# A fused transformer and state-space kernel: where the weighted values and the first out products of a group stand between the gate's halves

## The chip, the cores and the metric

The kernel runs on one core of a Trainium2 chip. The metric is the device time of the whole program in microseconds (us), as the median of three runs. The engines are named as in the profile: PE is the matrix engine (PEld its weight loads), DVE the vector engine, ACT the scalar engine, POOL the GpSimd engine, SP the engine that issues nearly all DMAs. Each engine has its own instruction queue and works it off in order; engines wait for each other by semaphores.

## The reference, cut to what matters

Four residual layers on 1024 tokens of 512 features: attention, a gated feed-forward layer, a Mamba-2 mixer, and the feed-forward layer again. The change touches only the mixer:

```python
def _L0_attn_b_ref(input_states, in_proj_w, conv_w, conv_b, dt_bias, A_log, D, norm_w, out_w):
    H, P, N, G, K = (128, 64, 128, 8, 4)
    INTER = H * P                                    # 8192 channels
    proj = input_states @ in_proj_w.T
    gate, xBC, dt = ...                              # split of proj
    xBC = silu(conv(xBC) + conv_b)                   # 4 taps along the tokens
    hs, Bm, Cm = ...                                 # values, keys, queries (8 groups)
    y = _ssd(hs, -exp(A_log), Bm, Cm, D, dt, dt_bias)
    g = y * silu(gate)
    gg = g.reshape(b, l, G, INTER // G)
    g = gg * rsqrt(mean(gg * gg, -1) + EPS) * norm_w # one norm for each group
    return g @ out_w.T
```

The kernel computes `_ssd` for each sequence of 256 tokens as a masked, decayed attention: (C B^T, times a decay of the two positions) times (dt x), plus D x.

## The kernel before, in words

The mixer's 8192 channels are 64 blocks of 128 channels (two heads each), in 8 groups g of 8 blocks. Block i is number gi = i mod 8 of its group. All tiles have channels on the 128 partitions and the 1024 tokens (4 sequences of 256) along the free axis. Every product with weights is made of three matmuls per slice of 128 features (`mm3`, L110, matmuls at L115 to L117), since each operand is split into a high and a low part (`split`: ACT casts at L107, the other engine subtracts at L108).

A block does this:

- `projected("x", i)` (L1127): 24 matmuls into a PSUM tile `pp`, in two halves of 512 tokens with 12 matmuls each. Between the halves it calls the function `between`, which is empty for x. `pp` has two buffers, used in turn by the x and the gate of each block.
- `conv` (L961): ACT scales the last tap into `acc`, DVE adds three taps (L971), ACT applies silu (L975). The result is `x2`, with two buffers.
- `projected("g", i, between)`: the gate's two halves, with `between` in the middle; ACT writes silu of it into `gt` (L1204), which has one buffer.
- `differences` (L999) for two heads: the decay factors `em` (four buffers, so two blocks' worth), made of DVE (L1004), POOL (L1008) and ACT (L1013 to L1016) work from rows `r` that SP loads.
- `turned` (L1022): eight PE transposes of `x2` into `trx` (L1027), and DVE multiplies by dt into `xd` (L1030).
- `weighted` (L1019): DVE multiplies `em` by the group's masked scores `gm` (L1020).

What needs all this comes one block later. `inner_products(i - 1)` (L1160) gives the weighted values of the block before: `product` (32 matmuls into `pyy`, L1044), and `gated` (DVE adds D x and multiplies by the gate, L1054 and L1057; SP stores the result to DRAM as `spill`, L1059; ACT squares it, L1066; POOL adds the square to the group's sum `sq`, L1067). The square is written into the block's `x2`, so that buffer is free for the convolution two blocks on only when POOL has read it.

Once a group: `scores` (L978) is a generator. Its first step makes the tile `gm`; each of the next four makes the scores of one sequence, with two products on PE (L986 and L990, each shown as two matmuls) into a tile `pg`, and a masking multiply by DVE into `gm` (L991).

The out products of group g are made during group g+1, for 8 tiles of 128 tokens. `recall` (L1097) loads half the group's stored values for one tile from DRAM (`gr`) and splits it into `gh`, which has three buffers; two recalls make a tile. `outer` (L1150) makes 24 matmuls (`pog`), 12 with each half; for the first tile (t = 0) it also computes the norm with `root` (L1085: 16 small matmuls `pqs`, a square root on ACT at L1093, a reciprocal on DVE at L1094); then DVE adds the scaled result to `x` (`scaled`, L1115). `PER` says how many tiles are recalled at the end of the block before block gi.

`pog`, `pqs`, `pg` and `trx` all come from one PSUM pool of two buffers (L797, tag "m").

From block 8 on PE's order is exactly that of the program text, written out by hand (`manual_schedule`, L1227). For the other engines the framework's planner orders the instructions: it goes by the order of the text, but puts a later instruction ahead where an earlier one is not ready by its own plan. What it decides is fixed when the program is built.

In the first block of a group (gi = 0, g > 0) PE's order before the change is: x; the scores of two sequences; first half of the gate; the scores of the other two; the weighted values of the block before; second half of the gate; transposes. In the second block: x; the out product of t = 0 with its norm; the weighted values; the out product of t = 1; both halves of the gate; transposes. Blocks 2 to 7: x; one out product; the weighted values; the gate; transposes (and, in two of them, the projection of the next group's B or C).

Of the kernel before, what the change touches and what calls it, by code (L numbers as in the profile page):

```python
# [79 lines left out]
def hybrid_kernel(  # L80
# [705 lines left out]
    def mixer(feed, later):  # L786
        with ExitStack() as es, ExitStack() as inner:
# [173 lines left out]
            def conv(pp, ch, tag, bufs):  # L961

                acc = (po_ if tag == "gb" else p2).tile([P, NT], F32, name="acc", tag=tag, bufs=bufs)
                nc.scalar.activation(  # L964
                    acc, pp, AF.Identity, bias=cb_s[:, ch : ch + 1], scale=cw_s[:, ch, 3:4]
                )
                av = acc.rearrange("p (b t) -> p b t", b=B)
                pv = pp.rearrange("p (b t) -> p b t", b=B)
                for tap in range(3):
                    d = 3 - tap  # L970
                    nc.vector.scalar_tensor_tensor(  # L971
                        av[:, :, d:], pv[:, :, : L - d], cw_s[:, ch, tap : tap + 1], av[:, :, d:],
                        ALU.mult, ALU.add,
                    )
                silus.append(nc.scalar.activation(acc, acc, AF.Silu).ins)  # L975
                return acc

            def scores(bt, ct):  # L978

                gm = p2.tile([P, B, 3, P], F32, name="gm", tag="gm", bufs=1)  # L980
                yield gm
                for b in range(B):
                    pg = ps.tile([P, 3, P], F32, name="pg", tag="m")
                    k0, k1 = bt[:, b * L : b * L + P], bt[:, b * L + P : (b + 1) * L]
                    q1 = ct[:, b * L + P : (b + 1) * L]
                    nc.tensor.matmul(  # L986
                        pg[:, 0:2, :].rearrange("p s i -> p (s i)"), k0, ct[:, b * L : (b + 1) * L],
                        start=True, stop=True,
                    )
                    nc.tensor.matmul(pg[:, 2, :], k1, q1, start=True, stop=True)  # L990
                    nc.vector.tensor_tensor(gm[:, b], pg, tri.rearrange("p (s i) -> p s i", s=3), ALU.mult)  # L991
                    yield

            def rows(h):
                r = p2.tile([P, NT], F32, name="r", tag="r", bufs=2)
                load(r, cumd[h : h + 1, :].to_broadcast([P, NT]))
                return r
# [40 lines left out]
            def product(xd, es2):  # L1038
                py = ps_y.tile([P, B, L], F32, name="pyy", tag="pyy")
                for b in range(B):  # L1040
                    for k in range(2):
                        for hh in range(2):
                            d = slice(hh * PD, (hh + 1) * PD)
                            nc.tensor.matmul(  # L1044
                                py[d, b, k * P :], xd[:, 2 * b + k, d],
                                es2[hh][:, b, 2 * k : 2 if k == 0 else 3, :].rearrange("p s i -> p (s i)"),
                                start=(k == 0), stop=(k == 1),
                            )
                return py

            def gated(n, x2, gt, py, sq):

                gb = po_.tile([P, NT], F32, name="gb", tag="gb", bufs=3)
                nc.vector.scalar_tensor_tensor(  # L1054
                    gb, x2, dh[:, n : n + 1], py.rearrange("p b t -> p (b t)"), ALU.mult, ALU.add
                )
                nc.vector.tensor_tensor(gb, gb, gt, ALU.mult)  # L1057
                if n < NB - 1:
                    load(spill[(n // GB) % 2][n % GB], gb)  # L1059
                else:  # L1060
                    last.append(gb)
                if sq is None:
                    sq = p2.tile([P, NT], F32, name="sq", tag="sq")
                    nc.scalar.activation(sq, gb, AF.Square)
                else:
                    nc.scalar.activation(x2, gb, AF.Square)  # L1066
                    (nc.gpsimd if n < NB - 1 else nc.vector).tensor_tensor(sq, sq, x2, ALU.add)  # L1067
                return sq
# [16 lines left out]
            def root(sq):  # L1085
                pq = ps.tile([P, TT], F32, name="pqs", tag="m")
                for t in range(TT):
                    nc.tensor.matmul(
                        pq[:, t : t + 1], sq[:, t * P : (t + 1) * P], ones[:, 0:1], start=True, stop=True
                    )  # L1090
                rg = rg_s.pop(0)
                rg_s.append(rg)
                nc.scalar.activation(rg, pq, AF.Sqrt, bias=eps, scale=1.0 / (GB * P))  # L1093
                nc.vector.reciprocal(rg, rg)  # L1094
                return rg
# [13 lines left out]
            def partial(po, g, hl, half):  # L1109
                ks = range(half * 4, half * 4 + 4)  # L1110
                mm3(po, [[v[:, k % 4, :] for v in hl] for k in ks], [wos[g][k] for k in ks],
                    half == 0, half == 1)

            def scaled(g, t, po):
                nc.vector.scalar_tensor_tensor(  # L1115
                    x[:, t, :], po, rgs[g][:, t : t + 1], x[:, t, :], ALU.mult, ALU.add
                )
# [32 lines left out]
            def outer():  # L1150

                q, t, hl = recalled.pop(0)
                po = ps.tile([P, C], F32, name="pog", tag="m")
                for half in range(2):
                    partial(po, q, hl[half], half)
                if t == 0:
                    rgs[q] = root(sqs.pop(q))
                scaled(q, t, po)

            def inner_products(m):  # L1160
                px2, gt, xd, em = stage.pop(m)
                py = product(xd, em)
                sqs[m // GB] = gated(m, px2, gt, py, sqs.get(m // GB))
# [3 lines left out]
            scoring = scores(group["b"], group["c"])  # L1167
# [3 lines left out]
            rr = {h: rows(h) for h in range(2)}  # L1171
            stage, sqs, wos, rgs, todo = {}, {}, {}, {}, []
            recalled = []
            PER = {1: 2, 2: 1, 3: 1, 4: 1, 5: 1, 6: 1, 7: 1}
            def block(i, scoring, gm):
                g, gi = divmod(i, GB)
                x2 = conv(projected("x", i), i, "x2", 2)
                if gi == 0 and g:

                    scoring = scores(group["b"], group["c"])  # L1180
                    gm = next(scoring)
                    next(scoring)
                    next(scoring)
                    todo.extend((g - 1, t) for t in range(TT))
                outers = len(recalled)
                if outers:
                    outer()
                if i and (outers or g == 0):
                    inner_products(i - 1)
                while recalled:  # L1190
                    outer()
                if gi == 7:
                    wos.setdefault(g, []).extend(out_weights(g, k) for k in range(4))

                def between():

                    for _ in scoring:
                        pass
                    if not outers and g:
                        inner_products(i - 1)  # L1200

                pp = projected("g", i, between)
                gt = p2.tile([P, NT], F32, name="gt", tag="gt", bufs=1)
                nc.scalar.activation(gt, pp, AF.Silu)  # L1204
                em = []
                for h in (2 * i, 2 * i + 1):
                    with tc.issue_after(silus[2]) if i == 0 else ExitStack():
                        em.append(differences(h, rr.pop(h)))
                    if h + 2 < H:
                        rr[h + 2] = rows(h + 2)  # L1210
                xd = turned(i, x2)
                if gi in NEXT and g + 1 < G:
                    convolved(NEXT[gi], g + 1)
                for e in em:
                    weighted(e, gm)
                stage[i] = (x2, gt, xd, em)
                for _ in range(PER.get(gi + 1, 0)):
                    if todo:
                        q, t = todo.pop(0)
                        recalled.append((q, t, [recall(q, t, half) for half in range(2)]))  # L1220
                if gi == 7:
                    wos[g].extend(out_weights(g, k) for k in range(4, 8))
                return scoring, gm

            for i in range(GB):
                scoring, gm = block(i, scoring, gm)
            with tc.manual_schedule(engines={nc.tensor.engine}):  # L1227
                for i in range(GB, NB):
                    scoring, gm = block(i, scoring, gm)
# [122 lines left out]
```

## Time and profile before

| what | value |
|---|---|
| median of three runs | 1916.23 us (1913.35 to 1919.33) |
| the profiled execution's own time | 1920.11 us |
| its span, first to last instruction | 1918.3 us |
| PE busy | 1819.3 us |
| DVE busy | 1468.6 us |
| ACT busy | 1462.1 us |
| POOL busy | 389.3 us |
| mean granted PE clock | 0.978 |

The span is the time from the first to the last instruction of one profiled execution. "Busy" leaves out waits, register work and the issuing of DMAs. Rows of a timeline give the start, the duration, the engine, the line, the operation, the tile written and the tiles read, and in brackets the idle time before it with what ended it. Matmuls overlap: a 512-column matmul is listed with 0.39 us, but one starts every 0.23 us. Group 2 (blocks 16 to 23, from 730.6 us) serves as the example below; its first block ends its x projection at 736.15 us.

### The profile page before, as it was taken

To read this page: it belongs to the slowest core of one execution; us is meant where nothing else is said; L and a number is where in the kernel's file an instruction comes from. 1 tells how busy PE (TensorE), PEld (TensorE's weight loads), DVE (VectorE), ACT (ScalarE), POOL (GpSimd) and SP (SyncE) were. 2 spreads that over 40 slices of the span, in tenths; PEclk is the share of its full clock that TensorE was granted. 3 is DMA by queue.
4 is the path that set the end of the run, shared out by engine and by line. 5 is a ranking of instruction groups with operands and counts; after the bars stand their busy time and mean duration, and the time that the engine had idled before them with its cause. 6 is when DMAs were issued, how large, how long until landed. Compare 5 with 4: busy or idle time off the path is not lost.

```text
span 1918.3 us, 29873 instructions
## 1 busy us (share of the span) xinstructions
PE 1819.3 (95%) x10706; PEld 1465.5 (76%) x10706; DVE 1468.6 (77%) x2304; ACT 1462.1 (76%) x2877; POOL 389.3 (20%) x393
## 2 busy tenths in 40 slices
PE   8999989899989999999999989999999999999997
PEld 6777767677767887888788878877788788778776
DVE  5566667789997788778877787878777877777767
ACT  5666675379987888787878787887788788778753
POOL 6332230024411112121211111111111121111100
PEclk8999999899999999999999999999999999999999
DMA  4000000034554445444544454445445544554241
GB/s 141 1 1 1 22 15 25 24 111 154 182 180 160 159 143 175 149 151 125 192 148 154 137 177 140 162 144 171 148 143 165 165 143 143 163 167 149 94 139 49
DMA packets 152773, 240.35 MB, mean 125 GB/s; under 512 B 12464, under 2 KB 77616, under 8 KB 152624
## 3 DMA queue, kind: packets, MB, share of 16 engines
q1 hardware_dynamic: 152624, 238.44, 38.6%
q8 instruction: 84, 1.38, 0.3%
q14 instruction: 65, 0.53, 0.1%
HBM read 202.75 MB, written 35.65 MB: 124 GB/s over the span
## 4 chain that ended last, share of the span: by engine, by line
PE 74%; ACT 10%; DVE 8%; DMA 3%; POOL 2%; issue 2%; SPq 0%; DVEq 0%; ACTq 0%; POOLq 0%
PE pp L115 12%; PE pp L116 11%; PE pp L117 11%; PE pyy L1044 8%; PE pog L115 6%; PE pog L117 6%; PE pog L116 6%; PE trx L1027 2%; ACT e L477 2%; DMA wor<-in_wout_dram 2%; DVE acc L971 1%; POOL sq L1067 1%; PE ptr L493 1%; PE pq L115 1%; PE pq L116 1%
## 5 line engine op out<-in xcount | busy, mean ns | idle before, releaser
L115 PE MATMUL pp<-mx,w 128*128 128x512 f32 (+1 forms) x1160 | 464.2, 400 | 3.2 <-DVE acc L971 1.1
L117 PE MATMUL pp<-mx,w 128*128 128x512 f32 (+1 forms) x1160 | 452.5, 390 | 0.0
L116 PE MATMUL pp<-mx,w 128*128 128x512 f32 (+1 forms) x1160 | 452.4, 390 | 0.0
L971 DVE SCALAR_TENSOR_TENSOR acc<-pp,cw_s,acc 128x1012 f32<-128x1012 f32 (+2 forms) x240 | 304.4, 1271 | 18.4 <-ACT acc L964 16.7
L1020 DVE TENSOR_TENSOR em<-em,gm 128x1536 f32<-128x1536 f32 x128 | 241.5, 1888 | 73.7 <-ACT em L1016 73.7
L115 PEld LDWEIGHTS pp<-mx,w 128*128 128x128 f32 x1160 | 218.9, 189 | 55.9 <-issue 9.7
L117 PEld LDWEIGHTS pp<-mx,w 128*128 128x128 f32 x1160 | 218.6, 188 | 46.2 <-issue 0.7
L116 PEld LDWEIGHTS pp<-mx,w 128*128 128x128 f32 x1160 | 219.2, 189 | 40.8 <-issue 0.6
L1008 POOL TENSOR_SCALAR_AFFINE_SELECT r<-r 128x512 f32<-128x512 f32 x128 | 94.8, 741 | 759.9 <-DMA r<-cumd 587.8
L115 PE MATMUL pog<-wo,gh 128*128 128x512 f32 x512 | 207.0, 405 | 30.1 <-ACT gh L107 28.3
L1067 POOL TENSOR_TENSOR sq<-sq,acc 128x1024 f32<-128x1024 f32 x55 | 152.7, 2776 | 374.3 <-ACT acc L1066 374.3
L117 PE MATMUL pog<-wo,gh 128*128 128x512 f32 x512 | 204.7, 400 | 0.6 <-DVE gh L108 0.6
L116 PE MATMUL pog<-wo,gh 128*128 128x512 f32 x512 | 204.3, 399 | 0.0
L1044 PE MATMUL pyy<-em,xd 128*64 128x128 f32 (+1 forms) x2048 | 183.7, 329 | 1.3 <-DVE em L1020 1.0
L1044 PEld LDWEIGHTS pyy<-em,xd 128*64 128x64 f32 x2048 | 130.1, 137 | 57.6 <-issue 17.6
L1013 ACT ACTIVATE em<-r,col_t 128x128 f32<-128x128 f32 x512 | 170.5, 390 | 0.8
L1016 ACT ACTIVATE em<-r,col_t 128x128 f32<-128x128 f32 x512 | 166.3, 389 | 0.2
L1004 DVE TENSOR_SCALAR em<-r,col_t 128x128 f32<-128x128 f32 x512 | 138.8, 328 | 22.8 <-PE pyy L1044 18.4
L108 DVE TENSOR_TENSOR w<-wr,w 128x512 fp32r<-128x512 f32 x126 | 93.3, 740 | 65.9 <-ACT w L107 65.9
L115 PEld LDWEIGHTS pog<-wo,gh 128*128 128x128 f32 x512 | 98.9, 193 | 55.0 <-ACT gh L107 31.2
L107 ACT CAST w<-wr 128x512 fp32r<-128x512 f32 x144 | 88.6, 616 | 64.7 <-PE pp L116 61.9
L107 ACT CAST gh<-gr 128x512 fp32r<-128x512 f32 (+1 forms) x128 | 76.4, 607 | 69.2 <-PE pog L116 55.9
(290 smaller groups left out, 3310.5 us busy)
## 6 DMA issues: line engine op xcount, KB each, us to landing
wr<-in_win_dram SPq DMA_DIRECT2D x287, 256.0 KB, 2.8
r<-cumd SPq DMA_DIRECT2D x128, 512.0 KB, 3.9
spill<-gb SPq DMA_DIRECT2D x63, 512.0 KB, 2.6
gr<-spill SPq DMA_DIRECT2D x120, 256.0 KB, 2.9
wor<-in_wout_dram SPq DMA_DIRECT2D x64, 256.0 KB, 3.0
out_dram<-x SPq DMA_DIRECT2D x8, 256.0 KB, 2.3
x<-in_x_dram SPq DMA_DIRECT2D x1, 1536.0 KB, 9.9
gr<-spill SPq DMA_DIRECT2D x8, 192.0 KB, 2.5
```

The source lines that it names most:

```text
L107: nc.scalar.copy(hl[0], v)
L115: nc.tensor.matmul(o, lh, rh, start=(first and k == 0), stop=False)
L116: nc.tensor.matmul(o, lh, rl, start=False, stop=False)
L117: nc.tensor.matmul(o, ll, rh, start=False, stop=(last and k == n - 1))
L971: nc.vector.scalar_tensor_tensor(av[:, :, d:], pv[:, :, : L - d], cw_s[:, ch, tap : tap + 1], av[:, :, d:], ALU.mult, ALU.add,)
L1004: nc.vector.tensor_scalar(e[:, b, 2, :], rv[:, b, 1, :], col_t[:, h, b, 1:2], 0.0, ALU.subtract, ALU.min,)
L1008: nc.gpsimd.affine_select(rv[:, :, 0, :], rv[:, :, 0, :], pattern=[[0, B], [1, P]], compare_op=ALU.is_ge, fill=-1e30, base=0, channel_mult ...
L1013: nc.scalar.activation(e[:, b, 1, :], rv[:, b, 1, :], AF.Exp, bias=col_t[:, h, b, 2:3])
L1016: nc.scalar.activation(e[:, b, 0, :], rv[:, b, 0, :], AF.Exp, bias=col_t[:, h, b, 0:1])
L1020: nc.vector.tensor_tensor(e, e, gm, ALU.mult)
L1044: nc.tensor.matmul(py[d, b, k * P :], xd[:, 2 * b + k, d], es2[hh][:, b, 2 * k : 2 if k == 0 else 3, :].rearrange("p s i -> p (s i)"), sta ...
L1067: (nc.gpsimd if n < NB - 1 else nc.vector).tensor_tensor(sq, sq, x2, ALU.add)
```

## The change

In the first two blocks of groups 1 to 7 (`late`), nothing stands between x and the first half of the gate any more. Between the gate's halves of the first block stand the scores of two sequences, the weighted values of the block before, and the scores of the other two sequences. Between the gate's halves of the second block stand the weighted values of the first, and behind them the out product of t = 0. The second block's end recalls two tiles instead of one, the first block's end one instead of two, so the third block has two out products, around its weighted values.

```diff
-            PER = {1: 2, 2: 1, 3: 1, 4: 1, 5: 1, 6: 1, 7: 1}
+            PER = {1: 1, 2: 2, 3: 1, 4: 1, 5: 1, 6: 1, 7: 1}
             def block(i, scoring, gm):
                 g, gi = divmod(i, GB)
                 x2 = conv(projected("x", i), i, "x2", 2)
                 if gi == 0 and g:
-
                     scoring = scores(group["b"], group["c"])
                     gm = next(scoring)
-                    next(scoring)
-                    next(scoring)
                     todo.extend((g - 1, t) for t in range(TT))
-                outers = len(recalled)
-                if outers:
-                    outer()
-                if i and (outers or g == 0):
-                    inner_products(i - 1)
-                while recalled:
-                    outer()
+
+
+                late = gi < 2 and g > 0
+                if not late:
+                    if recalled:
+                        outer()
+                    if i:
+                        inner_products(i - 1)
+                    while recalled:
+                        outer()
                 if gi == 7:
                     wos.setdefault(g, []).extend(out_weights(g, k) for k in range(4))
 
                 def between():
-
+                    if late:
+                        if gi == 0:
+                            next(scoring)
+                            next(scoring)
+                        inner_products(i - 1)
+                        while recalled:
+                            outer()
                     for _ in scoring:
                         pass
-                    if not outers and g:
-                        inner_products(i - 1)
 
                 pp = projected("g", i, between)
```

## The prediction, made before the changed kernel was run

> **What bounds the kernel now.** I read the page's busy line first, then PE's list of waits, then PE's timeline over one group's first two blocks, then the other engines over the same stretch.
>
> ```profile
> PE 1819.3 (95%) x10706; PEld 1465.5 (76%) x10706; DVE 1468.6 (77%) x2304; ACT 1462.1 (76%) x2877; POOL 389.3 (20%) x393
> PE pog L115 <- ACT gh L107: 28.3, 7, 4.8
> PE pg L986 <- DVE gm L991: 4.5, 6, 0.9
> ```
>
> PE is the bound. In the list of waits (engine and tile, what ended the wait, us in total, times, longest) the first place goes to seven waits of the out products for `gh`, one in each of groups 1 to 7; six waits of the scores stand second. Both lie in the blocks that the change reorders. PE's timeline of group 2:
>
> ```profile
> 740.66 0.38 PE L990 MATMUL pg<-acc 128*128 128x128 f32 x2
> 741.77 0.70 PE L986 MATMUL pg<-acc 128*128 128x256 f32 x2 [0.72 <-DVE gm L991]
> 742.30 0.38 PE L990 MATMUL pg<-acc 128*128 128x128 f32 x2
> 742.62 2.82 PE L1044 MATMUL pyy<-em,xd 128*64 128x256 f32 x32
> ...
> 757.07 0.39 PE L117 MATMUL pog<-wo,gh 128*128 128x512 f32 x1
> 761.32 0.50 PE L115 MATMUL pog<-wo,gh 128*128 128x512 f32 x1 [3.87 <-ACT gh L107]
> ...
> 763.33 0.63 PE L117 MATMUL pog<-wo,gh 128*128 128x512 f32 x1
> 763.76 0.63 PE L115 MATMUL pog<-wo,gh 128*128 128x512 f32 x1
> ...
> 766.03 1.84 PE L1088 MATMUL pqs<-ones,sq 128*128 128x1 f32 x16
> ```
>
> The second half of the first out product waits 3.87 us, and then matmuls start every 0.43 us instead of every 0.23. The stretches before, in and after the wait show why (stretch, length, busy times, then the granted clock):
>
> ```profile
> 757.30:761.30 4.00, 0.15 (x1) 0.00 (x0) 3.79 (x8) 3.97 (x6) 0.00 (x0) 1.00 0.50 171
> 761.30:765.50 4.20, 4.18 (x11) 2.96 (x12) 4.20 (x7) 4.03 (x10) 1.13 (x1) 0.62 0.77 243
> ```
>
> The clock is granted at about half for some 3.5 us behind the wait. From 754.57 to 766.03 this out product takes 11.46 us; undisturbed ones take 5.53. What is late is the group's own last block: its products end at 745.4, DVE finishes `gb` at 751.36, the spill lands at 753.96, the recall at 756.69, and ACT casts at 760.66 to 761.27, being held until then:
>
> ```profile
> 751.51 1.04 ACT L1066 ACTIVATE acc<-gb 128x1024 f32<-128x1024 f32 x1
> 753.87 1.03 ACT L1204 ACTIVATE gt<-pp 128x1024 f32<-128x1024 f32 x1
> 757.11 1.20 ACT L964 ACTIVATE acc<-pp,cb_s,cw_s 128x1024 f32<-128x1024 f32 x1 [2.21 <-POOL sq L1067]
> 760.66 1.12 ACT L107 CAST gh<-gr 128x512 fp32r<-128x512 f32 x2
> ```
>
> **What is removed.** PE does the same matmuls; the gain can only be waits and slow clock. The first out products of groups 1 to 7 take 11.21, 11.46, 11.37, 12.32, 11.83, 11.80 and 12.53 us. Less 5.53 each that is 5.68 + 5.93 + 5.84 + 6.79 + 6.30 + 6.27 + 7.00 = **43.8 us**: 28.9 idle (the row's 28.3, and 0.6 for DVE's low part), the rest slow clock. The third and fourth scores take 2.39 us in group 2 (740.23 to 742.62) and 1.39 in group 1, where they wait for nothing; 1.0 in each of six groups is **6.1 us** (group 4 has 1.16). Together 49.9.
>
> **The new order against the old times.** I lay PE's new order out without waits for group 2, from the end of x at 736.15, with durations from the same timeline: gate half 2.85, two scores 1.23, weighted values 2.75, two scores 1.39, gate half 2.88, transposes 0.79, x 5.54, gate half 2.85, weighted values 2.75, out product 2.76 + 2.77, norm sums 1.77, gate half 2.88. This gives the time at which PE will ask for each thing; beside it I set when the trace of before has it ready. That assumes that the other engines keep their times, a cautious reading, since the weighted values of block 15 end at 742.98 instead of 745.37.
>
> - Second scores, asked at 742.98: need the first masking multiplies. Before, DVE did the first 0.4 us after its scores, but the second only at 741.72. Bounds 0 to 1.0 a group (the wait of today); I take 0.3, since 2.75 us of weighted values lie between.
> - Gate half of block 17, asked at 753.58: needs the `pp` buffer of block 16's gate, which ACT releases with `gt` at 754.90. The two gate projections were 14.6 us apart in ordinary blocks (0.8 + 5.5 + 5.5 + 2.75) and are now 6.3. Bounds: 0 if `gt` follows the earlier `gb`, 1.3 in this group (up to 2.3 in group 7) if ACT keeps its order. I take 0.7.
> - Weighted values of block 16, asked at 756.43: the second multiply by `gm` ends at 754.22. 2.2 us of cover; before, 13.6.
> - Out product's second half, asked at 761.94: cast at 761.27. 0.7 to spare, plus whatever the earlier `gb` and the gate's wait add. **The 3.87 us wait is covered even if ACT does not move**, by a gate half and the weighted values (5.6 us) that now run ahead. Taken at nothing; were that cover gone, the old 5.9 come back.
> - Transposes, asked at 769.36: they use both "m" buffers, so `scaled` of the out product must be done within the 2.88 us of the gate half. Square root 0.27, reciprocal 0.20, `scaled` 0.74 sum to 1.2; before it took 6.1 us (767.80 to 773.87), 2.8 of them DVE idle ahead of the next weighted values, which now come first. Bounds 0 to 2.8; I take 0.5.
> - Third block, two out products: the stores they recall are long on DRAM; before, the t = 1 tile ran with no wait. The move takes two recall DMAs (256 KB each), four splits and one `scaled` along. In SP's queue the `wr` and `r` loads behind the recalls come forward; POOL's square sum and the block 17 convolution behind it start no later. Cost nothing: the blocks after it leave DVE 4 us in 20 idle (16.10 and 15.47 busy in two stretches of 20.2).
>
> New waits are 1.5 us a group, 10.5 in seven. They are too short for the half clock, by the 0.72 us row, after which nothing slows.
>
> **Two rules beside the rows.** The Trainium skill (GPSIMD Engine Reference, 8. Key points) says that GpSimd shares its SBUF interfaces with VectorE and contends with DVE instructions in a two-port mode or with two SBUF inputs. That speaks against the change: the square sum on POOL moves towards the multiplies by `gm`, the tightest cover above.
>
> ```profile
> 752.70 4.37 POOL L1067 TENSOR_TENSOR sq<-sq,acc 128x1024 f32<-128x1024 f32 x1 [6.83 <-ACT acc L1066]
> 752.47 1.75 DVE L1020 TENSOR_TENSOR em<-em,gm 128x1536 f32<-128x1536 f32 x1
> 754.74 3.40 DVE L1004 TENSOR_SCALAR em<-r,col_t 128x128 f32<-128x128 f32 x6
> L1020 DVE TENSOR_TENSOR em<-em,gm x128: 1742/1751/3015, 425.0 to 1813.4; 128x1536 f32<-128x1536 f32 x128
> ```
>
> Six 128-column pieces of `em` take 3.40 beside the square sum, 1.2 undisturbed; a multiply takes 3.0 at most instead of 1.75. By the row the multiply ends at 755.5, cost 0. By the rule at its worst (held for all 4.4 us, from 750.3) it ends at 756.5, 0.1 us late. I take 0.
>
> The other is TensorE: Matmul & The Clock Gate, Part 1: half clock only after an idle window of about 3.4 us. Here group 1 has a wait of 3.04 us (transposes for ACT's silu, 559.95 to 562.99), and the clock is 0.66 from 563 to 567; the next x takes 7.18 instead of 5.55. The row decides: a new wait of 3 us costs 1.6 more (7 × 4.6 = 32 instead of 7 × 3.0 = 21). That wait itself hangs on DVE and ACT work that the change leaves, and I let it stand.
>
> **Sum.** −43.8 − 6.1 + 10.5 = −39.4. On the profiled execution's 1920.1 that gives 1880.7. It lies 0.2% above the runs' median, so I apply the difference to the median: 1916.2 − 39.4 = **1877**.
>
> **Rivals.**
> 1. All new waits are covered since ACT and DVE follow the earlier weighted values: −49.9, 1866. For it: 2.4 us of lead. Against: DVE has 40.8 and ACT 39.5 busy us from 736.15 to 782.38, and PE will pass through that in about 7 us less than 46.2.
> 2. The planner leaves ACT's casts of `gh` behind later work, about 4 us later than now: the half is 2 us late with 1.9 of slow clock, which leaves 7.1 − 1.5 − 4.0 = 1.6 a group, −11, 1905. For it: the casts already stand behind a convolution that waits for POOL. Against: the recall stands ahead of that in the text.
> 3. **Slower**: DVE's planner puts block 17's three taps ahead of the second multiply of block 16. They wait for ACT and POOL and end at 764.23; the multiply then ends at 765.9, 9.5 us late, with 2.1 of slow clock. 7.1 saved against 11.6 lost is +4.5 a group, +31, 1948. It decides from a multiply that ends 5 us late, at 761.4. Against: the multiply stands ahead in the text and the trace keeps that order.
> 4. The waits only move and add up to about the same; PE's order does change, so this needs an accident.
>
> **Chances.** The forecast (1867 to 1892) 0.55; rival 1 at 0.17; rival 2 (1892 to 1910) 0.14; no change within 0.3%, 5.7 us, which is about what can be told from none, 0.04; slower 0.10. Faster is 0.86. The range runs from 1862 (rival 1 with group 1's 3 us wait gone) to 1905, in rival 2; its own case alone would give 1867 to 1892.
>
> **What would show it.** Right: the out products' waits for `gh` gone from the list; first out products at 5.5 us and the clock whole behind them; short waits at the second block's gate for `gt` (L1204) and at its transposes; group period 5 to 7 us shorter. Wrong: waits of `pyy` for `em` (L1020) above 3 us in the second block, or `gh` waits still there.

## The result, and the profile after

The changed kernel takes **1885.71 us** (median of four runs, 1883.82 to 1887.02), beside 1915.66 for the kernel before in the same session; the ratio is 0.9841, with a 95% interval of 0.9823 to 0.9859. That is 30 us faster, where 39 were forecast, and inside the forecast's 1867 to 1892. The profiled execution took 1886.09 us with a span of 1884.3 and a mean granted clock of 0.987.

The page's busy line, and the four lines of PE's list of waits that the change touches (engine and tile, what ended the wait, us in total, times, longest), of the kernel after:

```profile
PE 1805.5 (96%) x10706; PEld 1454.6 (77%) x10706; DVE 1475.8 (78%) x2304; ACT 1470.4 (78%) x2883; POOL 385.5 (20%) x393
PE pg L986 <- DVE gm L991: 14.4, 7, 4.6
PE trx L1027 <- DVE gm L991: 2.1, 5, 1.0
PE trx L1027 <- ACT rg L1093: 1.4, 1, 1.4
PE trx L1027 <- DVE x L1115: 1.2, 4, 0.4
```

The line of the out products that wait for `gh`, 28.3 us in seven waits, is gone. The scores that wait for their masking multiplies have taken its place: seven waits again, but half the time. Of the transposes' lines those for `rg` and `x` are new; the one for `gm` had one wait of 1.1 us before, ahead of the blocks that changed, and it is still there. PE's busy time fell by 13.8 us for the same 10706 matmuls: that part of the gain is slow clock that no longer follows the waits.

PE's timeline of group 2 after (start, duration, engine, line, tiles, and in brackets the idle time before it and what ended it); its first x projection ends at 730.77:

```profile
734.14 0.60 PE L986 MATMUL pg<-acc 128*128 128x256 f32 x2
734.58 0.39 PE L990 MATMUL pg<-acc 128*128 128x128 f32 x2
734.89 2.82 PE L1044 MATMUL pyy<-em,xd 128*64 128x256 f32 x32
739.18 0.70 PE L986 MATMUL pg<-acc 128*128 128x256 f32 x2 [1.47 <-DVE gm L991]
...
744.15 0.66 PE L1027 MATMUL trx<-con,acc 128*128 128x128 f32 x4 [0.20 <-DVE gm L991]
...
752.93 2.82 PE L1044 MATMUL pyy<-em,xd 128*64 128x256 f32 x32
755.68 0.50 PE L115 MATMUL pog<-wo,gh 128*128 128x512 f32 x1
...
761.26 1.84 PE L1088 MATMUL pqs<-ones,sq 128*128 128x1 f32 x16
```

The first out product runs from 755.68 to 761.26 without a gap: 5.58 us, where it took 11.46. In the other six groups it takes 5.57 to 5.58 too. The one gap of weight is the third score's (the first of the second pair), behind the weighted values.

**Where the 34.0 us between the two spans lie.** I cut the trace at the end of the transposes of each group's last block and of the next group's third block, which holds all that the change moves. The seven stretches sum to 507.5 us before and 478.9 after: −28.6. Another 5.0 lie ahead of block 8, where the orders of PE, ACT and DVE are the same in all kernels of this study; that point comes anywhere from 537.1 to 545.8 us in them, so I don't count it to the change. (By the trace's record of the clock, it stands at half for 41.0 us up to there before and for 30.7 after, and half of that difference is about the 5.0.) Laid out without any wait, the seven stretches would take 453.3. So waits and the slow clock behind them took 54.2 us of them before and 25.6 after. Below, "stretch sum" always means the sum of these seven, each time of one profiled execution.

### The profile page after: what moved, and what is told of

Its sections match the earlier page's. It is cut to its first block, busy times and chain, and to the rows that moved or that the text cites. A ratio compares the mean times of both kernels' runs of the same rounds, so it can differ in the third digit from the quotient of the medians.

```text
span 1884.3 us, 29891 instructions
## 1 busy us (share of the span) xinstructions
PE 1805.5 (96%) x10706; PEld 1454.6 (77%) x10706; DVE 1475.8 (78%) x2304; ACT 1470.4 (78%) x2883; POOL 385.5 (20%) x393
## 4 chain that ended last, share of the span: by engine, by line
PE 73%; DVE 12%; ACT 8%; DMA 3%; issue 3%; POOL 1%; SPq 0%; DVEq 0%; ACTq 0%; POOLq 0%
PE pp L115 11%; PE pp L116 11%; PE pp L117 11%; PE pyy L1044 7%; PE pog L115 6%; PE pog L117 6%; PE pog L116 6%; PE trx L1027 2%; ACT e L477 2%; DVE em L1020 2%; DVE acc L971 1%; DMA wor<-in_wout_dram 1%; PE ptr L493 1%; PE pq L115 1%; PE pq L116 1%
## 5 line engine op out<-in xcount | busy, mean ns | idle before, releaser
L115 PE MATMUL pp<-mx,w 128*128 128x512 f32 (+1 forms) x1160 | 464.2, 400 | 3.1 <-DVE acc L971 1.1
L117 PE MATMUL pp<-mx,w 128*128 128x512 f32 (+1 forms) x1160 | 452.8, 390 | 0.0
L971 DVE SCALAR_TENSOR_TENSOR acc<-pp,cw_s,acc 128x1012 f32<-128x1012 f32 (+2 forms) x240 | 304.8, 1272 | 21.3 <-ACT acc L964 19.4
L1020 DVE TENSOR_TENSOR em<-em,gm 128x1536 f32<-128x1536 f32 x128 | 249.2, 1952 | 54.6 <-ACT em L1016 54.6
L115 PEld LDWEIGHTS pp<-mx,w 128*128 128x128 f32 x1160 | 219.5, 189 | 53.7 <-issue 7.5
L1008 POOL TENSOR_SCALAR_AFFINE_SELECT r<-r 128x512 f32<-128x512 f32 x128 | 105.5, 825 | 749.0 <-DMA r<-cumd 616.5
L117 PEld LDWEIGHTS pp<-mx,w 128*128 128x128 f32 x1160 | 219.1, 189 | 46.6 <-issue 0.7
L1067 POOL TENSOR_TENSOR sq<-sq,acc 128x1024 f32<-128x1024 f32 x55 | 139.0, 2528 | 359.7 <-ACT acc L1066 359.7
L115 PE MATMUL pog<-wo,gh 128*128 128x512 f32 x512 | 201.7, 394 | 1.3 <-DVE x L1115 0.8
L116 PE MATMUL pog<-wo,gh 128*128 128x512 f32 x512 | 199.6, 390 | 0.0
L117 PE MATMUL pog<-wo,gh 128*128 128x512 f32 x512 | 199.4, 390 | 0.0
L1004 DVE TENSOR_SCALAR em<-r,col_t 128x128 f32<-128x128 f32 x512 | 135.7, 318 | 21.8 <-PE pyy L1044 17.8
L477 ACT ACTIVATE e<-sc,nmx 128x256 f32<-128x256 f32 (+1 forms) x256 | 104.2, 442 | 21.0 <-DVE nmx L471 20.9
```

Source lines behind the costliest of these rows:

```text
L115: nc.tensor.matmul(o, lh, rh, start=(first and k == 0), stop=False)
L116: nc.tensor.matmul(o, lh, rl, start=False, stop=False)
L117: nc.tensor.matmul(o, ll, rh, start=False, stop=(last and k == n - 1))
L477: nc.scalar.activation(es_[c][:, 2 * j + pr, :], sc[:, j, :], AF.Exp, bias=nm[:, j : j + 1], accum_out=rs[:, c, h : h + 1],)
L971: nc.vector.scalar_tensor_tensor(av[:, :, d:], pv[:, :, : L - d], cw_s[:, ch, tap : tap + 1], av[:, :, d:], ALU.mult, ALU.add,)
L1004: nc.vector.tensor_scalar(e[:, b, 2, :], rv[:, b, 1, :], col_t[:, h, b, 1:2], 0.0, ALU.subtract, ALU.min,)
```

## The experiments

The first question is which half of the change removes the wait for `gh`. The expectations weigh two accounts. A: what counts is that PE asks later, which the second block's order brings. B: the recalled values must also come earlier, which the first block's order brings. The diffs are cut to the lines that matter. Those of kernels described as parts of the whole change are against the kernel after, the others against the kernel that the text names.

**Second block alone.** The first block is as before (two scores ahead of the gate, two inside, then the weighted values); the second block and the recalls are as after.

```diff
                     gm = next(scoring)
+                    next(scoring)
+                    next(scoring)
...
-                    if late:
-                        if gi == 0:
-                            next(scoring)
-                            next(scoring)
+                    if late and gi == 0:
+                        for _ in scoring:
+                            pass
+                        inner_products(i - 1)
+                    elif late:
                         inner_products(i - 1)
```

> Edit: the first block of a group as before (two scores ahead of the gate, the other two and the weighted values between its halves), the second block and the recalls as after. Theory A (the gain is the cover of the recall in the second block): the first out product takes 5.5 us in all seven groups, 43.8 us less than before; the third score waits about 1.0 us in six groups as before; about 0.3 us a group at the transposes. About 41 us under before, some 1875 us, so below the changed kernel by about 10. Rival B (the change needs the first block's earlier weighted values to have the stored group early): a wait of 1 to 2 us for gh or for the gate's buffer stays in each second block, about 28 us under before, 1888 us.

Measured: 1887.78 us, ratio 0.9832 [0.9815, 0.9848], stretch sum 479.3. The wait for `gh` is gone. ACT's cast ends 25.5 us behind the first x and DVE's low part at 26.3, as late as in the kernel before; PE asks at 28.0. So A's mechanism is shown: the cover alone suffices, with ACT where it was. The time is not A's 1875, since new waits take part of the gain back: the gate's half for `gt` 3.8 us, the second block's transposes 5.2. The scores' 4.8 us and group 1's 3.5 for silu stand much as before. The gate's wait for `gt`, which was forecast for the changed kernel and is absent there, does exist in this one.

**First block alone.** The first block is as after, the second block and the recalls as before.

```diff
-            PER = {1: 1, 2: 2, 3: 1, 4: 1, 5: 1, 6: 1, 7: 1}
+            PER = {1: 2, 2: 1, 3: 1, 4: 1, 5: 1, 6: 1, 7: 1}
...
-                late = gi < 2 and g > 0
+                late = gi == 0 and g > 0
```

> Edit: the first block as after, the second block and the recalls as before (out product, weighted values, out product, gate). Theory A: the out product's second half still waits for gh, by 3.9 less the 2.2 us that gb is earlier, some 1.7 us with little slow clock; the third score's wait grows to 1.5 us (4.6 in group 1). Between 10 and 20 us under before, about 1900 us. Rival B: most of the gain is here, 28 us under before, 1888 us.

Measured: 1881.36 us, 0.9802 [0.9781, 0.9823], stretch sum 472.2: a little better than the whole change, and far from the 1900 or so of A. The wait for `gh` is gone here too, with nothing moved ahead of the out product. In groups 2 to 7 PE asks 22.3 to 23.4 us behind x; the low part is done at 21.65 to 22.8. The margin is small, and part of it is a wait: PE asks later than the 21.3 us of before because it has waited 1.5 to 2.2 us for the third score.

**The smallest edit.** In the kernel before, only the weighted values and the last two scores inside the first block's gate change places.

```diff
                 def between():

-                    for _ in scoring:
-                        pass
                     if not outers and g:
                         inner_products(i - 1)
+                    for _ in scoring:
+                        pass
```

> Edit: the kernel before with one swap: in the first block's gate the weighted values come first and the last two scores behind them. Theory A: gb no longer stands behind two masking multiplies and what they wait for, it ends 2 to 3 us earlier, and ACT's cast follows ahead of the second block's convolution as in the run with the first block alone: the out product's wait under 1 us, no slow clock; the third score waits for nothing; between 35 and 45 us under before, 1877 us. Rival (the two scores behind half the gate are what brings the cast forward): the wait stays over 2 us with slow clock, 1900 us.

Measured: 1877.36 us, 0.9790 [0.9762, 0.9818], stretch sum 468.6. The `gh` line is gone. The lines of PE's waits that bear on the change:

```profile
PE trx L1027 <- DVE gm L991: 10.3, 13, 2.4
PE pog L115 <- ACT rg L1093: 1.8, 2, 1.0
```

One swap of two statements gives more than the whole change. So **each half removes the wait by itself**, and the gains do not add: the second half about 32 us, the first 38, both 30 (in the stretches 28, 35 and 29).

**What the first half does.** The weighted values of the block before end 6.9 us behind the first x projection instead of 9.2; the cast ends 5.5 us earlier. Times in group 2, from the end of the first x projection:

| | before | after |
|---|---|---|
| DVE ends `gb` | 15.2 | 12.9 |
| the spill lands | 17.8 | 15.5 |
| the recall lands | 20.5 | 18.35 |
| ACT has cast the second half | 25.1 | 19.6 |
| DVE has its low part | 25.85 | 21.65 |
| PE asks for it | 21.3 | 27.9 |

Up to the recall, everything is 2.2 to 2.3 us earlier. Then ACT gains another 3.3: in the kernel before, the casts stand behind the second block's convolution, and in the new order one stands ahead of it. ACT's timeline of the kernel after:

```profile
749.75 0.60 ACT L107 CAST gh<-gr 128x512 fp32r<-128x512 f32 x1
750.26 0.62 ACT L107 CAST w<-wr 128x512 fp32r<-128x512 f32 x1
750.78 1.20 ACT L964 ACTIVATE acc<-pp,cb_s,cw_s 128x1024 f32<-128x1024 f32 x1
```

That suggested a third account, C: the planner's order on ACT is all that the first half brings. Three kernels put it to the test.

**ACT's order alone.** The kernel before, with the second block's convolution queued on ACT behind the cast of the first out product's second half.

```diff
-        nc.scalar.copy(hl[0], v)
+        casts.append(nc.scalar.copy(hl[0], v).ins)
...
-                x2 = conv(projected("x", i), i, "x2", 2)
+                ppx = projected("x", i)
+                with tc.issue_after(wanted.pop()) if wanted else ExitStack():
+                    x2 = conv(ppx, i, "x2", 2)
...
                         recalled.append((q, t, [recall(q, t, half) for half in range(2)]))
+                        if t == 0:
+                            wanted.append(casts[-1])
```

> Edit: the kernel before, PE's order untouched; only on ACT the second block's convolution is queued behind the cast of the first tile's second half of gh, instead of ahead of it. Theory C (the wait of the out product is ACT's order: the recall lands 20.5 us after x ends, PE needs it at 21.3, and the cast is held till 24.5 by a convolution that waits for POOL's square sum, a cast, a table load and an exponential): the cast ends near 21.2, the out product waits under 1 us and keeps its clock, the third score waits 1.0 us as before; 35 to 42 us under before, 1879 us. Theory A (it is the place of the matmuls: the values come late to DRAM and PE asks too early): the out product still waits over 2 us with slow clock, 1900 us or more.

Measured: 1917.64 us (ten runs, 1904.8 to 1931.7), 1.0005 [0.9979, 1.0031], stretch sum 509.8: no gain. PE's timeline in its group 2 (this kernel's lines are two higher: L117 is L115, L119 is L117):

```profile
751.52 0.50 PE L117 MATMUL pog<-wo,gh 128*128 128x512 f32 x1 [2.10 <-ACT gh L109]
...
753.41 0.50 PE L119 MATMUL pog<-wo,gh 128*128 128x512 f32 x1 [1.15 <-DVE gh L110]
```

and ACT's and DVE's at the same place:

```profile
750.33 0.63 ACT L1016 ACTIVATE em<-em 128x512 f32<-128x512 f32 x1 [0.99 <-DVE em L1006]
750.87 0.60 ACT L109 CAST gh<-gr 128x512 fp32r<-128x512 f32 x1
...
751.00 1.74 DVE L1022 TENSOR_TENSOR em<-em,gm 128x1536 f32<-128x1536 f32 x1
752.67 1.28 DVE L110 TENSOR_TENSOR gh<-gr,gh 128x512 fp32r<-128x512 f32 x2
```

The cast no longer stands behind the convolution, but behind an exponential that waits for DVE; DVE then has a multiply ahead of the low part. One wait of 3.9 us has become two of 2.1 and 1.15. In all seven stretches PE now stands for 29.2 us instead of 36.4, but the clock is at half for 54.6 us instead of 37.5, and that takes the rest back. So this order on ACT without the earlier data is worth nothing. It brought the cast forward by 1.8 us only (25.1 to 23.35 us behind x), where C asked for 3.9; what a cast at once on landing would bring is not shown.

**The earlier data without ACT's order.** The first-block kernel, with the recall and casts of the first out product's second half made behind the second block's convolution, and those of t = 1 moved there as well. (`firsts` collects ACT's first instruction of each convolution; the diff shows what differs from the first-block kernel.)

```diff
                 x2 = conv(projected("x", i), i, "x2", 2)
+                if gi == 1 and g:
+                    with tc.issue_after(firsts[-1]):
+                        recalled[0][2].append(recall(*recalled[0][:2], 1))
+                    recalled[1][2].extend(recall(*recalled[1][:2], half) for half in range(2))
...
-                        recalled.append((q, t, [recall(q, t, half) for half in range(2)]))
+                        recalled.append((q, t, [recall(q, t, half) for half in range({0: 1, 1: 0}.get(t, 2))]))
```

> Edit: the first block alone as after (the run at 1881), with the recall of the first tile's second half, and of the second tile, put behind the second block's convolution in the text and on ACT. Theory C: the cast comes 2 to 4 us later than in that run, at 22.5 to 24 us from the end of x against 22.3 asked, and the wait is back, 1 to 2 us a group, partly with slow clock; 1890 to 1905 us. Theory A (the earlier weighted values are what counts): no wait above 0.5 us, within 4 us of 1881.

Measured: 1891.15 us, 0.9875 [0.9856, 0.9895], stretch sum 484.4. PE's waits show a wait for `gh` again:

```profile
PE pog L117 <- DVE gh L108: 6.8, 7, 1.4
```

The stretch sum is 12 us above that of the first block alone, of which 6.8 are these waits. They are short, and no slow clock follows them. Most of the rest is half clock behind the third score's waits, 13.7 us of it instead of 3.4, which the edit did not aim at. So of the 35 us that the first half gains in the stretches some two thirds stay without ACT's order, and ACT's order is what closes the last 1.4 us of the wait.

**The same move in the whole change.**

```diff
                 x2 = conv(projected("x", i), i, "x2", 2)
+                if gi == 1 and g:
+                    with tc.issue_after(firsts[-1]):
+                        recalled[0][2].append(recall(*recalled[0][:2], 1))
...
-                        recalled.append((q, t, [recall(q, t, half) for half in range(2)]))
+                        recalled.append((q, t, [recall(q, t, half) for half in range(2 if t else 1)]))
```

> Edit: the changed kernel with the same move of the recall's cast behind the second block's convolution. Both theories: PE asks at 27.8 us, so a cast at 22.5 to 24 is still in time; no wait for gh, within 5 us of the changed kernel's 1886. A wait for gh of 1 us or more would say that the second block's place gives no cover of its own.

Measured: 1882.00 us, 0.9831 [0.9811, 0.9850], stretch sum 474.1: no loss. In groups 5 to 7 the low part is done 24.0 us behind x and PE asks at 27.9. With both halves the cover is more than is needed, in line with the second block alone.

**What took the gain back.** The other question is the third score's wait. DVE's timeline of group 2 in the kernel after, over the time in which PE waits (from 737.7 on):

```profile
734.28 1.27 DVE L971 SCALAR_TENSOR_TENSOR acc<-pp,cw_s,acc 128x1016 f32<-128x1016 f32 x1
735.46 0.68 DVE L108 TENSOR_TENSOR w<-wr,w 128x512 fp32r<-128x512 f32 x1
736.06 0.75 DVE L1080 SCALAR_TENSOR_TENSOR wo<-wor,nw_s,wo 128x512 fp32r<-128x512 f32 x1
736.72 1.28 DVE L971 SCALAR_TENSOR_TENSOR acc<-pp,cw_s,acc 128x1020 f32<-128x1020 f32 x1
737.91 0.74 DVE L1080 SCALAR_TENSOR_TENSOR wo<-wor,nw_s,wo 128x512 fp32r<-128x512 f32 x1
738.57 1.02 DVE L991 TENSOR_TENSOR gm<-pg,tri 128x384 f32<-128x384 f32 x2
```

The first two scores are done by 735. Their masks (the masking multiplies, L991) come at 738.57, behind two taps, a weight split and two low parts of output weights (`wo`). The third score needs a buffer that the first mask releases. In group 1 the same queue is held by DMAs (windows of the kernel after: stretch, length, busy times of PE, PEld, DVE, ACT, POOL, then clock, DMA share, GB/s):

```profile
551.00:555.30 4.30, 0.04 (x1) 0.04 (x1) 3.33 (x6) 3.48 (x6) 0.00 (x0) 1.00 0.92 279
555.30:559.00 3.70, 3.70 (x11) 3.12 (x12) 3.48 (x5) 3.67 (x5) 0.63 (x1) 0.54 0.58 155
```

PE stands still for 4.3 us while the DMA engines are 92% busy: two of the output weights that ACT and DVE have ahead in their queues land only at 551.5 and 553.2. PE then gets half clock.

**Two scores ahead of the gate.** The whole change, with the first two scores back in front of the gate.

```diff
                     gm = next(scoring)
+                    next(scoring)
+                    next(scoring)
...
                     if late:
-                        if gi == 0:
-                            next(scoring)
-                            next(scoring)
                         inner_products(i - 1)
```

> Edit: as after, but two scores stand ahead of the gate's first half again; the weighted values and the other two scores between the halves. Theory A (the third score waits because DVE's masking multiplies stand behind taps and out weights in its queue once the scores come after half the gate): the multiplies have 5.6 us instead of 2.75 and DVE takes the first at once as before; the wait of 1.5 to 2.0 us (4.6 in group 1) falls to under 0.5. About 15 us under the changed kernel, 1870 us. Rival (DVE has simply too much work in this stretch, whatever the order): the wait moves to the fourth score, the transposes or the weighted values of the second block, and the time stays within 4 us of 1886.

Measured: 1880.83 us, 0.9804 [0.9789, 0.9818], stretch sum 472.9. The third score does not wait any more, but the transposes now wait for the masks, 9.1 us in ten waits against 2.1, and for `x` and `rg`, 6.5 against 2.6. The lateness moves to the next users of DVE's results, and the stretches fall by 6 us only.

**Half the output weights later.** The whole change, with the second four of the eight output weights of a group made behind the gate of the next group's first block, instead of at the end of the last block.

```diff
                 pp = projected("g", i, between)
+                if gi == 0 and g:
+                    wos[g - 1].extend(out_weights(g - 1, k) for k in range(4, 8))
...
-                if gi == 7:
+                if gi == 7 and g == G - 1:
                     wos[g].extend(out_weights(g, k) for k in range(4, 8))
```

> Edit: as after, but the second four out weights of a group (load, ACT scaling, DVE low part) stand behind the gate of the next group's first block instead of at the end of the last block. Theory A (DVE reaches the masking multiplies late because it stands at out weights that wait for their DMA): the third score's wait goes to under 0.5 us in all groups, 4.6 and the slow clock in group 1 included; 15 us under the changed kernel, 1871 us, unless the later weights make the out product of the second block wait. Rival (too much DVE work in the stretch): the same work only moves by some us, the time stays within 4 us of 1886.

Measured: **1866.28 us**, 0.9731 [0.9711, 0.9750], stretch sum 460.6, some 7 above the sum without waits. It is the fastest kernel of the study, 19 us below the change. Its line of PE's waits, and DVE's timeline at the same place of group 2:

```profile
PE pg L986 <- DVE gm L991: 5.7, 6, 2.2
```

```profile
728.09 0.68 DVE L108 TENSOR_TENSOR w<-wr,w 128x512 fp32r<-128x512 f32 x1
728.69 1.27 DVE L971 SCALAR_TENSOR_TENSOR acc<-pp,cw_s,acc 128x1020 f32<-128x1020 f32 x1
729.88 1.01 DVE L991 TENSOR_TENSOR gm<-pg,tri 128x384 f32<-128x384 f32 x2
```

Without the two `wo` in the way the masks start 1.3 us earlier against the scores, and the third score waits 0.21 us in this group instead of 1.47. Over all groups the scores' waits fall from 14.4 to 5.7 us, and the transposes of these blocks wait no more. The work is the same and only stands elsewhere, so its amount is not the cause. That shows the cause of most of the new wait: the output weights in DVE's and ACT's queues.

**Both together** (the two edits above in one kernel):

> Edit: as after, with two scores ahead of the gate again and the second four out weights behind the next group's gate. Theory A: no wait of the third score, and no wait of the transposes for the masking multiplies, since those waits were DVE standing at out weights; the three reordered blocks reach 65.2 us, their sum without waits, in every group; 4 us under the run with the weights alone, 1862 us. Rival (DVE has too much work in the stretch whatever stands where): the transposes keep waiting 0.9 us for the masks, 1872 us.

Measured: 1872.75 us, 0.9771 [0.9742, 0.9799], stretch sum 460.7. In the stretches it equals the kernel with the later weights alone. The 6 us between the two spans lie outside them: 2.0 ahead of block 8, 2.6 in the blocks behind the stretches, 1.3 behind the last block (an out product there waits 0.9 us for `wo`).

**The later weights without the cover.** The same move of the output weights (the diff of the later weights, line for line), first in the first-block kernel, then in the kernel before.

> Edit: the first block alone as after (the second block and the recalls as before), and the second four out weights behind the gate of the next group's first block. Theory A (the two parts of the change stand in for each other, and the out weights in DVE's queue make what is left): the third score's waits (1.5 us in six groups, 3.5 in group 1) fall as they did with the changed second block, 12 to 18 us under the first block alone; 1866 us, the same as with both blocks changed. Rival: the second block's cover is needed once the rest moves faster, the out product waits for gh again by 1 us or more a group, 1875 us.

> Edit: the kernel before, with nothing changed but the second four out weights, which stand behind the gate of the next group's first block. If the recall is late because DVE and ACT stand at out weights: gb and the cast come 2 to 3 us earlier, the out product waits 1 to 2 us instead of 3.9, mostly without slow clock, the third score by nothing; 25 to 30 us under before, 1888 us. If it is late because of where the weighted values and ACT's cast stand in the order: the wait stays at 3 us or more, 6 to 10 us under before, 1907 us.

Measured: the first-block kernel becomes 1885.40 us, 0.9828 [0.9799, 0.9857], stretch sum 475.4, where 1866 was expected. The kernel before becomes 1934.38 us (seven runs), 1.0078 [1.0055, 1.0100], stretch sum 526.9: **slower**, which no expectation held. PE's waits in the kernel before with this move:

```profile
PE pog L115 <- ACT wo L1079: 13.0, 8, 2.1
PE pog L115 <- ACT gh L107: 7.4, 7, 1.5
PE pog L116 <- DVE wo L1080: 3.4, 7, 0.7
```

The moved work is what the first out product reads next. Where nothing stands ahead of that product, it waits for `wo`. The expectation of the later weights in the whole change named that risk; these two did not.

But the waits are not what makes this kernel slower. In the seven stretches PE stands for 30.2 us, less than the 36.4 of before. What makes it slower is the clock, at half for 78.5 us instead of 37.5. In place of one wait of some 4 us the out product has several of 0.2 to 2.1, and half clock then stays for 10.2 us in five groups and 13.7 in two. In group 2 (the norm sums take 1.8 us at full clock):

```profile
760.47 0.50 PE L115 MATMUL pog<-wo,gh 128*128 128x512 f32 x1 [1.97 <-ACT wo L1079]
761.58 0.79 PE L116 MATMUL pog<-wo,gh 128*128 128x512 f32 x1 [0.60 <-DVE wo L1080]
763.88 3.41 PE L1088 MATMUL pqs<-ones,sq 128*128 128x1 f32 x16
```

and in windows (the clock is the third number from the end):

```profile
761.00:764.40 3.40, 2.82 (x9) 2.34 (x9) 3.40 (x5) 2.41 (x8) 0.00 (x0) 0.50 0.36 113
764.40:767.80 3.40, 3.40 (x18) 3.19 (x20) 1.42 (x2) 1.67 (x3) 0.49 (x1) 0.50 0.77 278
767.80:771.20 3.40, 3.40 (x26) 2.45 (x24) 0.02 (x1) 3.37 (x3) 0.14 (x1) 0.50 0.03 11
```

The half clock runs on through the norm sums and the weighted values, though PE is busy all the time there.

## Why the prediction was right, and where it was off

- **The wait removed.** Right, and for the reason given: covered even if ACT doesn't move, as the second block alone shows. The first out products fell to 5.58 us, with the clock whole behind them. What the prediction did not see is that the other half would be enough alone: it set the cast at its old time as a cautious reading and took the earlier weighted values for a reserve. They are worth the whole wait, with the small margin told above.
- **Second scores: the term that was mis-sized.** The prediction took 0.3 us a group, with 1.0 as the upper bound, since 2.75 us of weighted values lie between. Measured: 4.69, 1.54, 1.58, 1.72, 1.60, 1.64 and 2.10 us, every group above the bound. The bound was read from the kernel before, where DVE did its first mask 0.4 us after the scores. There a gate half lay between the pairs of scores; the prediction moved PE's scores and left DVE's queue in place beside them, without asking what would stand in it at that moment.
- **Half clock.** "They are too short for the half clock" was wrong in two groups. Behind the 4.69 us of group 1 it costs 1.6, behind the 2.03 us of group 7 some 1.5, and a third case follows below. The 0.72 us row could not carry the claim: the waits came out two to six times as long.
- **Gate half for `gt`.** Forecast 0.7 a group, measured nothing. ACT's silu ends 16.6 us behind x in group 2 and PE asks at about 19; the earlier `gb` and the third score's wait both help, as the prediction's lower bound allowed.
- **Transposes of the second block.** Forecast 0.5 a group, 3.5 in all; measured 1.8 in six groups, and 3.85 in group 1, with the slow clock behind it. Those of the first block wait 2.35 for the masks, which the sum did not hold.
- **Group 1's old 3 us wait for silu**, which the prediction let stand with its slow clock (4.7), is gone: PE is held earlier by the third score. Where the third score does not wait there, the wait is back: 3.5 us in the second-block kernel, 2.4 with both edits together.
- **POOL beside the multiplies.** No cost on PE, as forecast, but the row was read too mildly. In group 2 the multiply starts at 745.94, while the square sum runs (745.13 to 747.53), takes 3.2 us and ends 1.6 behind it. So it was held until the sum was done, which is the prediction's "rule at its worst"; it cost little because the sum took 2.4 us and not 4.4.

The terms side by side, in us over seven groups:

| term | predicted | measured |
|---|---|---|
| third score, with slow clock | 2.1 | 18.0 |
| gate half for `gt` | 4.9 | 0 |
| transposes, second block | 3.5 | 5.65 |
| transposes, first block | 0 | 2.35 |
| group 1's silu wait and slow clock, left standing | 4.7 | 0 |
| sum | 15.2 | 26.0 |

The measured sum agrees with the 25.6 of the stretches within what such readings are good for. The 10.8 us more than predicted are the difference between −39.4 and the −28.6 of the stretches. The −30 of the medians lies a little closer. That the total is not further off is in part luck: the third score alone cost 15.9 us more than predicted, and two terms of 9.6 us together came out at nothing.

## What to carry to other kernels

A wait for late data can be cured from either end, by asking later or by making it ready earlier; doing both pays once, and the smaller edit may be the better one. When PE's order is changed, lay out the queues of the engines that must answer in between, DVE's masks here, at the new moment: a bound read from the old order doesn't hold there. And before work is moved off a busy stretch, ask who reads its result next: the same move gave 19 us where the reader was covered and cost some 15 where it was not, there by half clock, with less waiting than before.

## What the hardware showed that I had not expected

The half clock can follow short waits. In group 1's second block PE stands for 1.36 and then 0.44 us with four transposes between, and the windows of the kernel after show full clock in that stretch and half in the next:

```profile
582.80:586.20 3.40, 1.60 (x12) 0.94 (x10) 1.80 (x5) 3.34 (x5) 0.00 (x0) 1.00 0.52 154
586.20:589.60 3.40, 3.40 (x10) 2.68 (x9) 2.05 (x4) 3.37 (x5) 0.00 (x0) 0.50 0.10 22
```

The x projection there takes 7.15 us instead of 5.54. The 2.03 us wait in group 7 was followed by a clock of 0.59 over three microseconds. Waits of 1.5 to 1.7 us in the five groups between had none behind them. By the rule of the Trainium skill that the prediction weighed (TensorE: Matmul & The Clock Gate, Part 1), with its idle window of about 3.4 us, neither should have slowed; the measurement decides.

The length of one wait is not what decides either. In the run with two scores ahead of the gate PE waits 2.46 us and soon after 0.88, and the clock stays whole:

```profile
554.10:557.50 3.40, 1.77 (x8) 1.13 (x6) 2.77 (x4) 3.33 (x5) 0.64 (x1) 1.00 0.89 280
557.50:560.90 3.40, 1.69 (x11) 1.39 (x12) 3.31 (x6) 3.37 (x5) 0.00 (x0) 1.00 0.67 260
560.90:564.30 3.40, 3.40 (x17) 2.81 (x16) 3.40 (x4) 3.37 (x5) 2.15 (x1) 1.00 0.85 249
```

In each of the 13 traces, the moments at which the clock changes lie whole multiples of 3.41 us apart. I cut the traces from 545 to 1800 us at these beats and added up PE's idle time in each piece at full clock. All 27 pieces with 1.97 us or more were followed by half clock, 7 of the 22 with 1.6 to 1.97, and of the 4653 with less only three. So what counts is the idle time within one beat: several waits add up, and a wait that lies across two beats can go free. The three exceptions, all in the first-block kernel with the later weights, hold 0.3 us of wait at most, but all 16 matmuls of the norm sums. Half clock also went on in every beat at half clock that held seven or more of these matmuls of one column (128x1). Why, no run here shows.

DVE instructions that run beside POOL's were not all stretched. In the kernel after (from 545 us on), 21 multiplies by `gm` (L1020) start while a POOL instruction runs; all 21 end 1.6 us behind the end of that instruction, so they were held, up to 3.2 us for 1.75. The 11 pieces of `em` (L1004) of this kind end 0.1 us behind it, up to 1.5 us for 0.28. Taps (L971), `gb` (L1054) and `xd` (L1030), which read PSUM, start beside POOL in 62 cases, and none took longer. Where the multiply was first, POOL's instruction grew instead: the prediction's rows of the kernel before show a square sum that starts 0.23 us behind a multiply and takes 4.37 us, where 2.4 is the shortest.
